# Graph layer on one core: the first twelve gathers read x itself, and messages run 16 instead of 22 units behind

## The chip, the cores and the metric

The kernel runs on one core of a Trainium2 chip. The metric is the time of one execution on the device in microseconds (us), lower is better; it is the median of several runs. Beside the times stands a profile of one execution: what each engine did when, and what ended each of its waits. The engines are TensorE (PE, its weight loads PEld), VectorE (DVE), ScalarE (ACT), GpSimd (POOL) and SyncE (SP, which here only issues DMAs).

## The reference

A pre-normalised graph layer over 6250 nodes with 256 features and 206250 edges (each with 64 features and a polarity). Edges are sorted by destination.

```python
h = relu(layernorm(x))                                   # [6250, 256]
e = relu(raw @ W_e1.T + b_e1) @ W_e2.T + b_e2            # [206250, 256]
edge_emb = (e * (clip(polarity, 0, 1) + 0.01)) @ W_le.T + b_le
msg  = relu(h[src] + edge_emb)
aggr = segment_sum(msg, dst, 6250)
t = (h + aggr) @ W_g1.T + b_g1
out = x + relu(layernorm(t) * ln_g + ln_b) @ W_g2.T + b_g2
```

All data are float32.

## The kernel before

Edges are taken in 403 blocks of 512; a block is two units of 256 edges, 806 units in all (`NU`). W_e2 and W_le are multiplied into one matrix once (`product`, L383), so that a unit costs the following.

- First layer, for a pair of blocks (four units): eight matmuls 64x512 into four PSUM banks (L248), emptied with bias and Relu by ACT (L257, three of them) and DVE (L254, the fourth).
- Second layer, for a unit (`edge_part`, L264): eight matmuls 128x256 (L272), emptied into a `msg` tile by DVE with the bias added (L277). In the prologue every third unit is `plain`: ACT empties it (L275), and the bias is added by DVE when the message is finished (L582).
- Gather: two indirect DMAs for each unit, issued by GpSimd (`gather`, L530, L537). Each fetches 128 rows of 1 KB from `hb_d`, a copy in HBM of relu(layernorm(x)) + b_le.
- Finishing the message (`whole`, L578): DVE multiplies `msg` by the polarity and adds the gathered row, in two instructions 128x256 (L584); ACT applies Relu in place (L589).
- Sums (`add_up`, L591): for each pair of blocks 32 matmuls (L601) with a 0/1 matrix `sel`, which DVE builds from the destinations (L566), add messages of equal destination. Later a further matmul distributes these sums to windows of 128 nodes, and the node layer follows (`node_work`).

The PSUM banks named `pz` come from a pool of seven (`psz`); every result above except the sums goes through it, in the order of the code.

The prologue (L342 to L446) loads x in 13 chunks of up to 512 rows on SP's queue, and for each chunk DVE takes row statistics (L140, L141), ACT a root (L365) and the normalisation with Relu (L375), GpSimd adds b_le (L379), and SP writes the rows to `hb_d` (L381). Since a gather may need any row, no gather starts before the last row is written. Between chunks the first `LEAD` = 22 units are put through both layers (`forward`), and their messages wait in `msg`.

The main loop runs over the units 22 to 805. In each pass a unit goes through the second layer, every fourth unit or pair of pairs brings first layers, sums and loads with it (`turn_of`), and `whole` is called for older units: the lag is `LEAD - u // SHRINK` units, never under one, so 22 at the start and 1 at the end. The order is written out by hand: no scheduler moves instructions, and each engine works through its own in the order of the code. Gathers are handed out in step with TensorE (`in_step`, L549): an estimate of TensorE's time so far, `spent`, divided by `STEP`, says how many may have been issued, each behind a matmul; besides, at most 16 units (`HG`) beyond the summed ones, for which there are buffers.

At the start of the loop a few steps are done once: `first_rows` (L456) and `rows_of_edges` (L464) work out the destinations relative to their strip, which `sel` needs; `row_numbers`, `stats_out` and `node_weights` follow some units later.

Of the kernel before, what the change touches and what calls it, by code (L numbers as in the profile page):

```python
# [17 lines left out]
P = 128  # L18
# [23 lines left out]
EDGE, LAYER, SUMS, NODES = 1.754, 0.9, 0.46, 0.65  # L42
STEP = 1.282
AFLOAT = 6.0
SHRINK = 36
HG = 16
FEW = 6
QUIET = (0, 1)
# [48 lines left out]
def gnn_kernel(ctx: ExitStack, tc: tile.TileContext, x, src_c, dst_c, dst_r, pol_c, raw_t, w_e1t, w_e2,  # L97
# [119 lines left out]
    with fast:  # L217
# [4 lines left out]
        e1_p = big.enter_context(tc.tile_pool(name="e1", bufs=8))  # L222
        msg_p = big.enter_context(tc.tile_pool(name="msg", bufs=LEAD + 2))
        psz = big.enter_context(tc.tile_pool(name="psz", bufs=7, space=PSUM))
        psd = big.enter_context(tc.tile_pool(name="psd", bufs=1, space=PSUM))
# [6 lines left out]
        def load_pair(q):  # L232
            if q < NP:
                raw[q] = ld.tile([P, 512], F32, name="raw")
                nc.sync.dma_start(out=raw[q], in_=raw_t[q])
# [68 lines left out]
        def forward(u):  # L304

            edge_part(u)
            if u % 4 == TURN:
                turn_of(u // 4)
# [12 lines left out]
        vecs = load("vecs", [P, 8], vec_c, nc.scalar)  # L321
        be1_s, be2_s, lng_s, lnb_s = (vecs[:, 2 * i:2 * i + 2] for i in range(4))
        load_pair(0)
        early = ExitStack()
# [9 lines left out]
        for j in range(S):  # L334
            nc.gpsimd.iota(p32[j * W:(j + 1) * W], pattern=[[0, 1]], base=0, channel_multiplier=1,
                           allow_small_or_imprecise_dtypes=True)
        full = NF * L * S
        dst_f = w0.tile([P, NT], F32, name="dst_f")
        be2_b = w0.tile([P, 2, P], F32, name="be2_b")


        with tc.tile_pool(name="p1", bufs=4) as p1, tc.tile_pool(name="p1x", bufs=11) as p1x:  # L342
            parts = list(chunks())
# [23 lines left out]
            def nodes_out(k):  # L367

                t0, p, t = parts[k]
                rs, nm = rs_s[:p, t0:t0 + t], nm_s[:p, t0:t0 + t]  # L370
                nc.vector.reciprocal(rs, rs)
                nc.vector.scalar_tensor_tensor(nm, mvs[k][:p, :t, 0], -1.0, rs, op0=ALU.mult, op1=ALU.mult)
                xt = xts.pop(k)
                for i in range(t):
                    nc.scalar.activation(xt[:p, i, :], xt[:p, i, :], AF.Relu, bias=nm_s[:p, t0 + i:t0 + i + 1],  # L375
                                         scale=rs_s[:p, t0 + i:t0 + i + 1])
                hb = p1.tile([P, CH, D], F32, name="hb")
                for i in range(t):
                    nc.gpsimd.tensor_add(hb[:p, i, :], xt[:p, i, :], ble_b[:p])  # L379
                for a, b in spread_out(p):  # L380
                    nc.sync.dma_start(out=rows(hb_d, t0, p, t)[a:b], in_=hb[a:b, :t])  # L381
# [37 lines left out]
            for k in range(len(parts) + 1):  # L419
# [15 lines left out]
                for _ in range((k > 0) + (k > 2 and k % 3 > 0)):  # L435
                    u = next(units, None)
                    if u is not None:
                        forward(u)
                if k in lists:
                    t, src = lists[k]  # L440
                    nc.scalar.dma_start(out=t, in_=src[:, :NT])
            nc.gpsimd.tensor_copy(dst_f, dst_f.bitcast(I32))
            for u in units:
                forward(u)
            nc.vector.tensor_scalar(pol_s, pol_s, 0.0, 1.0, op0=ALU.max, op1=ALU.min)
            nc.vector.tensor_scalar_add(pol_s, pol_s, 0.01)  # L446
# [74 lines left out]

        with tc.tile_pool(name="hg", bufs=HG) as hg_p, tc.tile_pool(name="ms", bufs=5) as ms_p, \
                tc.tile_pool(name="sel2", bufs=9) as sel2_p, tc.tile_pool(name="nd", bufs=3) as nd:
            got = 0
            acc = {}
# [4 lines left out]
            def gather(behind=None):  # L530
# [4 lines left out]
                if i == 0:  # L535
                    hg[u] = hg_p.tile([P, 2, D], F32, name="hg")
                g = nc.gpsimd.indirect_dma_start(  # L537
# [11 lines left out]
            def in_step(us, behind):  # L549

                nonlocal spent
                spent += us
                while got * STEP < spent + AFLOAT and got < 2 * min(NU, 4 * summed + HG):
                    gather(behind)
                    behind = None
# [22 lines left out]
            def whole(u):  # L578

                m = msg.pop(u)  # L580
                if plain(u):
                    nc.vector.tensor_add(m, m, bc_s)  # L582
# [156 lines left out]

            gathers(1)  # L740
            sums = add_pairs
            paced = in_step
            for i, fn in ((0, first_rows), (1, rows_of_edges), (3, lambda: rest.extend(select(0) + select(1))), (5, row_numbers), (6, stats_out),
                          (8, node_weights)):
                at(LEAD + i, fn)
# [4 lines left out]
            for u in range(LEAD, NU):  # L750
# [6 lines left out]
                piece()  # L757
                while made < u + 1 - max(LEAST, LEAD - u // SHRINK) - (by_two(u // 4) and (u + 1) % 8 == TURN):
                    gathers(made + 1)
                    whole(made)  # L760
                    made += 1
# [208 lines left out]
```

## Time and profile before

| | |
|---|---|
| median of 3 runs | 2550.69 us (2548.15 to 2566.38) |
| the profiled execution | 2558.52 us, its span 2556.8 us |
| granted TensorE clock, mean | 0.965 of full speed |
| busy: PE, DVE, POOL, ACT | 93%, 64%, 64%, 38% of the span |
| prologue, until the last rows are written | 0 to about 62 us |
| first gather issued | 63.65 us |
| first sums on TensorE (L601) | 97.99 us |
| one gather on GpSimd | 0.99 us, 1612 of them |

An engine's busy time is the union of its instructions' durations. In the profile's rows, the part in square brackets is the idle time of the engine just before the instruction and what ended it; "issue" means that the profile shows nothing that was waited for.

### The profile page before, as it was taken

To read this page: it belongs to the slowest core of one execution; us is meant where nothing else is said; L and a number is where in the kernel's file an instruction comes from. 1 tells how busy PE (TensorE), PEld (TensorE's weight loads), DVE (VectorE), ACT (ScalarE), POOL (GpSimd) and SP (SyncE) were. 2 spreads that over 40 slices of the span, in tenths; PEclk is the share of its full clock that TensorE was granted. 3 is DMA by queue.
4 is the path that set the end of the run, shared out by engine and by line. 5 is a ranking of instruction groups with operands and counts; after the bars stand their busy time and mean duration, and the time that the engine had idled before them with its cause. 6 is when DMAs were issued, how large, how long until landed. Compare 5 with 4: busy or idle time off the path is not lost.

```text
span 2556.8 us, 35901 instructions
## 1 busy us (share of the span) xinstructions
PE 2378.9 (93%) x12382; PEld 1670.3 (65%) x12382; DVE 1647.0 (64%) x3953; ACT 980.9 (38%) x1701; POOL 1638.7 (64%) x1675
## 2 busy tenths in 40 slices
PE   9998998999999989999999999999999999899987
PEld 7666666666666757666666666666666666666664
DVE  7776666666666666666656666656666666656655
ACT  7333333343343433334333433433333433333432
POOL 5666666666666666666666666666666665666662
PEclk9999999999999999998999999999999999999998
DMA  8433343334334433433343444334334333343341
GB/s 300 129 115 113 108 134 112 114 114 130 113 108 125 130 119 106 133 108 117 111 144 101 115 126 122 110 106 137 112 114 131 118 107 114 109 131 109 119 119 55
DMA packets 156084, 309.24 MB, mean 121 GB/s; under 512 B 33183, under 2 KB 77944, under 8 KB 155896
## 3 DMA queue, kind: packets, MB, share of 16 engines
q0 software_dynamic: 77376, 211.39, 28.5%
q1 hardware_dynamic: 77364, 92.23, 11.4%
q10 hardware_dynamic: 1156, 3.28, 0.3%
q8 instruction: 98, 1.61, 0.3%
q14 instruction: 90, 0.74, 0.1%
HBM read 293.92 MB, written 12.85 MB: 120 GB/s over the span
## 4 chain that ended last, share of the span: by engine, by line
PE 82%; issue 5%; DVE 5%; another core or an unknown queue 3%; ACT 1%; DVEq 0%; ACTq 0%
PE pz L272 49%; PE pz L248 17%; PE pd L601 9%; PE pz L701 3%; DVE hg L584 2%; PE pz L195 2%; PE pz L169 2%; DVE msg L277 1%; ACT e L257 0%; DVE sel L566 0%; PE pz L185 0%; ACT hg L589 0%; DVE hT L676 0%; DVE e L254 0%
## 5 line engine op out<-in xcount | busy, mean ns | idle before, releaser
L537 POOL DMA_INDIRECT hg<-hb_d,src_s x1612 | 1601.5, 993 | 861.2 <-issue 525.4
L272 PE MATMUL pz<-wc_s,e 128*128 128x256 f32 x6448 | 1486.5, 384 | 51.8 <-issue 38.6
L272 PEld LDWEIGHTS pz<-wc_s,e 128*128 128x128 f32 x6448 | 1216.7, 192 | 318.8 <-issue 99.8
L589 ACT ACTIVATE hg<-hg 128x512 f32<-128x512 f32 x805 | 508.5, 632 | 1117.2 <-DVE hg L584 854.1
L277 DVE TENSOR_TENSOR msg<-pz,bc_s 128x512 f32<-128x512 f32 x799 | 546.6, 686 | 325.1 <-PE pz L272 152.3
L584 DVE SCALAR_TENSOR_TENSOR hg<-msg,pol_s,hg 128x256 f32<-128x256 f32 x1612 | 697.5, 480 | 2.6 <-issue 1.5
L248 PE MATMUL pz<-raw,we_s 64*128 64x512 f32 x1612 | 510.3, 653 | 42.8 <-issue 22.9
L254 DVE TENSOR_SCALAR e<-pz,vecs 128x512 f32<-128x512 f32 x201 | 150.5, 749 | 500.0 <-PE pz L248 201.4
L257 ACT ACTIVATE e<-pz,vecs 128x512 f32<-128x512 f32 x605 | 376.4, 686 | 225.1 <-PE pz L248 84.9
L248 PEld LDWEIGHTS pz<-raw,we_s 64*128 64x128 f32 x1612 | 177.2, 195 | 281.6 <-issue 164.7
L601 PE MATMUL pd<-hg,sel 128*32 128x256 f32 x3216 | 258.6, 408 | 53.1 <-issue 50.9
L601 PEld LDWEIGHTS pd<-hg,sel 128*32 128x32 f32 x3216 | 114.0, 115 | 221.2 <-issue 170.0
L566 DVE SCALAR_TENSOR_TENSOR sel<-iota_w,zero_c,rel 128x128 f32<-128x128 f32 x403 | 138.8, 344 | 0.0
L613 ACT ACTIVATE ms<-pd 128x256 f32<-128x256 f32 x66 | 25.5, 386 | 191.7 <-remote 60.1
L701 PEld LDWEIGHTS pz<-s,ms 128*128 128x128 f32 x548 | 70.3, 194 | 9.1 <-issue 3.8
L701 PE MATMUL pz<-s,ms 128*128 128x128 f32 x548 | 71.7, 278 | 4.7 <-issue 2.5
L676 DVE SCALAR_TENSOR_TENSOR hT<-hT,zero_c,stb 128x128 f32<-128x128 f32 (+1 forms) x196 | 67.2, 343 | 1.7 <-issue 1.7
L169 PE MATMUL pz<-wg_s,hT 128*128 128x256 f32 (+1 forms) x196 | 52.8, 389 | 9.9 <-DVE hT L703 7.4
L195 PE MATMUL pz<-wg_s,nT 128*128 128x256 f32 (+1 forms) x196 | 53.9, 393 | 5.6 <-ACT hg L589 2.7
L169 PEld LDWEIGHTS pz<-wg_s,hT 128*128 128x128 f32 (+1 forms) x196 | 36.5, 191 | 20.0 <-DVE hT L703 9.7
L379 POOL TENSOR_TENSOR hb<-xt,rows_b 128x256 f32<-128x256 f32 (+1 forms) x49 | 34.2, 729 | 23.4 <-DMA xt<-in_x_dram 12.7
L195 PEld LDWEIGHTS pz<-wg_s,nT 128*128 128x128 f32 (+1 forms) x196 | 37.7, 195 | 15.2 <-issue 6.4
(91 smaller groups left out, 393.0 us busy)
## 6 DMA issues: line engine op xcount, KB each, us to landing
raw<-in_raw_t_dram SPq DMA_DIRECT2D x202, 256.0 KB
hg<-hb_d,src_s POOLq DMA_INDIRECT x1612
stb<-st_d SPq DMA_DIRECT2D x49, 128.0 KB
hb_d<-hb SPq DMA_DIRECT2D x12, 512.0 KB
xt<-in_x_dram SPq DMA_DIRECT2D x48, 128.0 KB
hT<-in_x_t_dram SPq DMA_DIRECT2D x48, 128.0 KB
out_dram<-ot SPq DMA_DIRECT2D x48, 128.0 KB
xt<-in_x_dram SPq DMA_DIRECT2D x11, 512.0 KB
```

Source lines behind the costliest of these rows:

```text
L169: nc.tensor.matmul(ph[:n, 0, :], aT[:, c, :n], wg1_s[:, c, :], start=c == 0 and not bias_by_pe, stop=c == 1)
L195: nc.tensor.matmul(po[:n, 0, :], nT[:, c, :n], wg2_s[:, c, :], start=c == 0, stop=c == 1)
L248: z = nc.tensor.matmul(pe[s, c], we1_s[s * F:(s + 1) * F, c * P:(c + 1) * P], raw[q][s * F:(s + 1) * F, :], start=True, stop=True)
L254: nc.vector.tensor_scalar(e1[b][:, c, :], pe[s, c], be1_s[:, c:c + 1], 0.0, op0=ALU.add, op1=ALU.max)
L257: nc.scalar.activation(e1[b][:, c, :], pe[s, c], AF.Relu, bias=be1_s[:, c:c + 1])
L272: last_z = nc.tensor.matmul(pz[:, i, :], e1[b][:, c, k:k + P], wc_s[:, c, :], start=c == 0, stop=c == 1)
L277: nc.vector.tensor_add(msg[u], pz, bc_s)
L537: g = nc.gpsimd.indirect_dma_start(out=hg[u][:, i, :], out_offset=None, in_=hb_d, in_offset=bass.IndirectOffsetOnAxis(ap=src_s[:, 2 * u + ...
L584: nc.vector.scalar_tensor_tensor(hg[u][:, i, :], m[:, i, :], pol_s[:, 2 * u + i:2 * u + i + 1], hg[u][:, i, :], op0=ALU.mult, op1=ALU.add)
L589: nc.scalar.activation(hg[u], hg[u], AF.Relu)
L601: z = nc.tensor.matmul(acc[g][j * W:(j + 1) * W, :], sel[g][:, k * S + j, :], m[:, j % 2, :], start=k == 0, stop=b == blocks_of(g)[-1])
L701: nc.tensor.matmul(pa[:, c, :n], ms[g][:, c * P:(c + 1) * P], box["sel2"][i][:, :n], start=i == 0, stop=i == len(gs) - 1)
```

## The change

- A small index tile `src_0` (12 columns of the source indices) is loaded on ACT's queue between `vecs` and `we2_s`. Before the first chunk is processed, GpSimd issues twelve gathers, those of units 0 to 5 (`RAW` = 6), that read rows of x and not of `hb_d`.
- Behind the last chunk, ahead of the units 20 and 21 of the prologue, DVE takes the statistics of the twelve gathered 128-row blocks; a root, a reciprocal and a product follow, and ACT normalises them in twelve instructions. When one of these six messages is finished, DVE adds b_le to the gathered rows in a further instruction, since `hb_d` would have held it.
- The lag is `LEAD - RAW - u // SHRINK` with `SHRINK` = 50: 16 units at the start and 1 at the end. In the first units of the loop two messages are finished in each pass (`ready_for`), until the lag is reached.
- The other gathers are counted from the thirteenth on, with `STEP` = 1.29.
- `rows_of_edges` and the call of `select` stand in one step, two units sooner than `select` stood before. The cast of the destinations on GpSimd moves from behind the last row addition to a place ahead of the last two.
- Buffers: half of the 16 gather buffers are allocated ahead of the prologue, x has ten chunk buffers instead of eleven, `hb` three instead of four, and the scratch of GpSimd's DMA descriptors is set to 8192 bytes for each partition; the kernel before leaves the default, twice as much.

```diff
@@ -40,10 +40,11 @@
 LEAD = 22
 LEAST = 1
 EDGE, LAYER, SUMS, NODES = 1.754, 0.9, 0.46, 0.65
-STEP = 1.282
+STEP = 1.29
 AFLOAT = 6.0
-SHRINK = 36
+SHRINK = 50
 HG = 16
+RAW = 6
 FEW = 6
 QUIET = (0, 1)
 TURN = 1
@@ -221,6 +222,7 @@
         sel_p = big.enter_context(tc.tile_pool(name="sel", bufs=3))
         e1_p = big.enter_context(tc.tile_pool(name="e1", bufs=8))
         msg_p = big.enter_context(tc.tile_pool(name="msg", bufs=LEAD + 2))
+        hx_p = big.enter_context(tc.tile_pool(name="hx", bufs=HG // 2))
         psz = big.enter_context(tc.tile_pool(name="psz", bufs=7, space=PSUM))
         psd = big.enter_context(tc.tile_pool(name="psd", bufs=1, space=PSUM))
         raw, sel, e1, hg, msg, ms = {}, {}, {}, {}, {}, {}
@@ -320,6 +322,11 @@
         nc.scalar.dma_start(out=we1_s, in_=w_e1t)
         vecs = load("vecs", [P, 8], vec_c, nc.scalar)
         be1_s, be2_s, lng_s, lnb_s = (vecs[:, 2 * i:2 * i + 2] for i in range(4))
+        src_0 = const.tile([P, 2 * RAW], I32, name="src_0")
+        mv_0 = const.tile([P, 2 * RAW, 2], F32, name="mv_0")
+        rs_0 = const.tile([P, 2 * RAW], F32, name="rs_0")
+        nm_0 = const.tile([P, 2 * RAW], F32, name="nm_0")
+        nc.scalar.dma_start(out=src_0, in_=src_c[:, :2 * RAW])
         load_pair(0)
         early = ExitStack()
         w0 = early.enter_context(tc.tile_pool(name="w0", bufs=1))
@@ -334,12 +341,19 @@
         for j in range(S):
             nc.gpsimd.iota(p32[j * W:(j + 1) * W], pattern=[[0, 1]], base=0, channel_multiplier=1,
                            allow_small_or_imprecise_dtypes=True)
+        for u in range(RAW):
+            hg[u] = hx_p.tile([P, 2, D], F32, name="hg")
+            for i in range(2):
+                nc.gpsimd.indirect_dma_start(
+                    out=hg[u][:, i, :], out_offset=None, in_=x,
+                    in_offset=bass.IndirectOffsetOnAxis(ap=src_0[:, 2 * u + i:2 * u + i + 1], axis=0))
         full = NF * L * S
         dst_f = w0.tile([P, NT], F32, name="dst_f")
         be2_b = w0.tile([P, 2, P], F32, name="be2_b")
 
 
-        with tc.tile_pool(name="p1", bufs=4) as p1, tc.tile_pool(name="p1x", bufs=11) as p1x:
+        with tc.tile_pool(name="p1", bufs=4) as p1, tc.tile_pool(name="p1h", bufs=3) as p1h, \
+                tc.tile_pool(name="p1x", bufs=AHEAD) as p1x:
             parts = list(chunks())
             xts, mvs = {}, {}
             units = iter(range(LEAD))
@@ -374,7 +388,7 @@
                 for i in range(t):
                     nc.scalar.activation(xt[:p, i, :], xt[:p, i, :], AF.Relu, bias=nm_s[:p, t0 + i:t0 + i + 1],
                                          scale=rs_s[:p, t0 + i:t0 + i + 1])
-                hb = p1.tile([P, CH, D], F32, name="hb")
+                hb = p1h.tile([P, CH, D], F32, name="hb")
                 for i in range(t):
                     nc.gpsimd.tensor_add(hb[:p, i, :], xt[:p, i, :], ble_b[:p])
                 for a, b in spread_out(p):
@@ -436,12 +450,23 @@
                     u = next(units, None)
                     if u is not None:
                         forward(u)
+                if k == 11:
+                    nc.gpsimd.tensor_copy(dst_f, dst_f.bitcast(I32))
                 if k in lists:
                     t, src = lists[k]
                     nc.scalar.dma_start(out=t, in_=src[:, :NT])
-            nc.gpsimd.tensor_copy(dst_f, dst_f.bitcast(I32))
-            for u in units:
+            for n, u in enumerate(units):
+                for m in range(n * RAW // 2, (n + 1) * RAW // 2):
+                    row_stats(p1, P, 2, lambda i: hg[m][:, i, :], mv_0[:, 2 * m:2 * m + 2, :])
                 forward(u)
+            nc.scalar.activation(rs_0, mv_0[:, :, 1], AF.Sqrt, bias=eps_t)
+            nc.vector.reciprocal(rs_0, rs_0)
+            nc.vector.scalar_tensor_tensor(nm_0, mv_0[:, :, 0], -1.0, rs_0, op0=ALU.mult, op1=ALU.mult)
+            for u in range(RAW):
+                for i in range(2):
+                    k = 2 * u + i
+                    nc.scalar.activation(hg[u][:, i, :], hg[u][:, i, :], AF.Relu, bias=nm_0[:, k:k + 1],
+                                         scale=rs_0[:, k:k + 1])
             nc.vector.tensor_scalar(pol_s, pol_s, 0.0, 1.0, op0=ALU.max, op1=ALU.min)
             nc.vector.tensor_scalar_add(pol_s, pol_s, 0.01)
 
@@ -519,9 +544,9 @@
             nc.vector.tensor_copy(bad_i, pq[:1, 0, 0:1])
 
 
-        with tc.tile_pool(name="hg", bufs=HG) as hg_p, tc.tile_pool(name="ms", bufs=5) as ms_p, \
+        with tc.tile_pool(name="hg", bufs=HG // 2) as hg_p, tc.tile_pool(name="ms", bufs=5) as ms_p, \
                 tc.tile_pool(name="sel2", bufs=9) as sel2_p, tc.tile_pool(name="nd", bufs=3) as nd:
-            got = 0
+            got = 2 * RAW
             acc = {}
             made = 0
             summed = 0
@@ -533,7 +558,7 @@
                 u, i = divmod(got, 2)
                 got += 1
                 if i == 0:
-                    hg[u] = hg_p.tile([P, 2, D], F32, name="hg")
+                    hg[u] = (hx_p if u % HG < HG // 2 else hg_p).tile([P, 2, D], F32, name="hg")
                 g = nc.gpsimd.indirect_dma_start(
                     out=hg[u][:, i, :], out_offset=None, in_=hb_d,
                     in_offset=bass.IndirectOffsetOnAxis(ap=src_s[:, 2 * u + i:2 * u + i + 1], axis=0))
@@ -550,7 +575,7 @@
 
                 nonlocal spent
                 spent += us
-                while got * STEP < spent + AFLOAT and got < 2 * min(NU, 4 * summed + HG):
+                while (got - 2 * RAW) * STEP < spent + AFLOAT and got < 2 * min(NU, 4 * summed + HG):
                     gather(behind)
                     behind = None
 
@@ -578,6 +603,8 @@
             def whole(u):
 
                 m = msg.pop(u)
+                if u < RAW:
+                    nc.vector.tensor_add(hg[u], hg[u], ble_b.rearrange("p (o d) -> p o d", o=1).to_broadcast([P, 2, D]))
                 if plain(u):
                     nc.vector.tensor_add(m, m, bc_s)
                 for i in range(2):
@@ -737,10 +764,14 @@
                 if fns:
                     todo.setdefault(now + 1, deque()).extendleft(reversed(fns))
 
-            gathers(1)
+            gathers(RAW + 1)
             sums = add_pairs
             paced = in_step
-            for i, fn in ((0, first_rows), (1, rows_of_edges), (3, lambda: rest.extend(select(0) + select(1))), (5, row_numbers), (6, stats_out),
+            def strips():
+                rows_of_edges()
+                rest.extend(select(0) + select(1))
+
+            for i, fn in ((0, first_rows), (1, strips), (5, row_numbers), (6, stats_out),
                           (8, node_weights)):
                 at(LEAD + i, fn)
             for i, fn in enumerate((by_group(0, ALU.max), by_group(1, ALU.min), by_row(0, ALU.max), by_row(1, ALU.min),
@@ -755,7 +786,9 @@
                     gathers(4 * summed + HG)
 
                 piece()
-                while made < u + 1 - max(LEAST, LEAD - u // SHRINK) - (by_two(u // 4) and (u + 1) % 8 == TURN):
+                lag = max(LEAST, LEAD - RAW - u // SHRINK) + (by_two(u // 4) and (u + 1) % 8 == TURN)
+                ready_for = min(u + 1 - lag, 2 * (u + 1 - LEAD))
+                while made < ready_for:
                     gathers(made + 1)
                     whole(made)
                     made += 1
@@ -958,7 +991,7 @@
 
         "x_t": laid(np.asarray(x).T.reshape(2, P, N).transpose(1, 0, 2)),
     }
-    nc = bacc.Bacc("TRN2", target_bir_lowering=False, num_devices=1)
+    nc = bacc.Bacc("TRN2", target_bir_lowering=False, num_devices=1, dynamic_dma_scratch_size=8192)
     arrays = {f"in_{k}_dram": a for k, a in ins.items()}
     args = [nc.dram_tensor(k, a.shape, mybir.dt.from_np(a.dtype), kind="ExternalInput").ap()
             for k, a in arrays.items()]
```

## The prediction

> **What bounds the kernel now.** I read the page's busy times and its chain first, then the table of ten-microsecond stretches around the place that is edited, then the timeline of VectorE there.
>
> ```profile
> PE 2378.9 (93%) x12382; PEld 1670.3 (65%) x12382; DVE 1647.0 (64%) x3953; ACT 980.9 (38%) x1701; POOL 1638.7 (64%) x1675
> ...
> PE 82%; issue 5%; DVE 5%; another core or an unknown queue 3%; ACT 1%; DVEq 0%; ACTq 0%
> ```
>
> TensorE sets the time: 93% busy, 82% of the chain that ended last. No other engine passes 64%, and all matrix products of the kernel remain in the changed one (equal instruction counts in the two built programs). So the change cannot shorten TensorE's work; it can only remove waits of TensorE or add some. Next, where are waits? Columns: stretch and length, then busy us (instructions) of PE, PEld, DVE, ACT, POOL, granted clock, DMA share, GB/s.
>
> ```profile
> 20.00:30.00 10.00, 10.00 (x46) 7.56 (x45) 9.03 (x34) 8.67 (x20) 7.57 (x12) 1.00 1.08 380
> 30.00:40.00 10.00, 10.00 (x47) 7.53 (x46) 9.35 (x32) 9.48 (x20) 7.83 (x12) 1.00 1.07 378
> 60.00:70.00 10.00, 10.00 (x46) 7.28 (x45) 6.12 (x9) 2.77 (x6) 6.65 (x5) 1.00 0.57 175
> 70.00:80.00 10.00, 10.00 (x46) 7.16 (x45) 8.68 (x16) 5.49 (x10) 7.90 (x7) 1.00 0.32 93
> 80.00:90.00 10.00, 10.00 (x49) 8.77 (x48) 6.33 (x18) 2.17 (x4) 7.58 (x8) 1.00 0.41 117
> 90.00:100.00 10.00, 7.23 (x32) 2.76 (x35) 7.10 (x16) 2.60 (x5) 5.69 (x6) 0.66 0.55 182
> 110.00:120.00 10.00, 9.92 (x44) 7.38 (x42) 9.93 (x24) 4.09 (x7) 7.73 (x8) 1.00 0.53 165
> ```
>
> TensorE is full up to 90 us, through the end of x's normalisation (near 62 us), the first gather (63.65 us) and the first finished message. A deep backlog of 22 units costs nothing there: there is no hole to fill. At 90 us comes a stall of TensorE's own: single matmuls 0.70 us apart, waiting for no engine. Such stalls return about every 26 us to the end, and weigh the same on both kernels.
>
> ```profile
> 8.11 1.97 PE L388 MATMUL pz<-wle_s,we_s 128*128 128x256 f32 x8 [1.22 <-DMA we_s<-in_w_e_dram]
> ...
> 61.14 0.69 DVE L277 TENSOR_TENSOR msg<-pz,bc_s 128x512 f32<-128x512 f32 x1 [2.76 <-PE pz L272]
> 62.87 0.69 DVE L277 TENSOR_TENSOR msg<-pz,bc_s 128x512 f32<-128x512 f32 x1 [1.03 <-PE pz L272]
> 64.82 0.75 DVE L254 TENSOR_SCALAR e<-pz,vecs 128x512 f32<-128x512 f32 x1 [1.26 <-PE pz L248]
> ...
> 77.31 1.66 DVE L584 SCALAR_TENSOR_TENSOR hg<-msg,pol_s,hg 128x256 f32<-128x256 f32 x4
> 78.89 0.69 DVE L277 TENSOR_TENSOR msg<-pz,bc_s 128x512 f32<-128x512 f32 x1
> ```
>
> The first line: TensorE waits for one weight load early. The others: VectorE has small holes between 57.69 and 78.89 us, 2.76 + 1.04 + 1.26 + 0.40 + 0.47 + 0.83 = 6.8 us in all (its ends against its next starts). 78.89 us is where it empties unit 26's PSUM bank.
>
> **The change, part by part.**
>
> *The index load.* The new load of `src_0` is third on ACT's queue. In the built order W_e2's load now stands where the `rows_b` load stood, behind a wait for the first load's completion lane. W_e2 was issued at 1.87 us; rows_b came out of that wait at 3.77. So W_e2 leaves 1.9 us later, and line 388 waits for it. Behind line 388 TensorE's work is gapless from 13.75 to 62.76 us but for some 0.5 us, so 1.4 to 1.9 us reach the end of the prologue. I take +1.9.
>
> *Twelve gathers at the start.* At 0.99 us busy and 0.30 between two (rows of L537), GpSimd needs 12 x 1.3 = 15.5 us from about 5 us on, so `hb` of chunk 0 (15.17 us before) starts near 21 to 23 us. One chunk takes 2.78 us of each 3.58 us, so 0.8 us is regained per chunk; with some 11 us idle between 15 and 60 us the delay of 6 to 8 us is gone before the last chunk, also with the 1.53 us cast moved ahead of the last two chunks. SP's row writes and raw loads queue behind those additions; raw pairs are loaded four pairs (36 us) ahead, which hides 8 us. Cost 0, and up to +2 if the last write slips. The bytes are 12 x 128 KB = 1.6 MB, 4.2 us at the 380 GB/s of a full stretch; x chunks (1.4 us each at that rate) are used every 3.6 us, so this is hidden.
>
> The Trainium skill, "DMA: Bandwidth & Descriptors", section "Queues, rings and completion order", says that each DMA engine takes turns between the queues that have work. That speaks against the early gathers: by it x's loads get half the rate while gathers are under way, an estimated 4 us of lost x transfer, and if that were not hidden the sum would be 4 us higher; the rows above (2.8 us per chunk at half rate, 3.6 us of use) hide it.
>
> *Statistics of twelve row blocks on VectorE.* Start to start a `bn_stats`/`bn_aggr` pair takes 0.55 us (8.27 to 8.83 us): 12 x 0.55 = 6.6, and 0.4 for reciprocal and product. ACT gets 12 x 0.52 = 6.2 us of Relu where it is a third busy.
>
> *Messages sooner.* In units 22 to 27 two messages per unit are finished instead of one. By unit 26's bank VectorE has finished messages 0 to 7, not 0 to 3: four more at 0.79 = 3.2, two more bias additions (units 4 and 7, L582) at 0.72 = 1.4. Messages 0 to 5 need an added 128x512 addition of `ble`, priced like L582: 6 x 0.72 = 4.3. The strips and the first seven `sel` blocks (0.26 to 0.35 each) now come ahead: 2.1.
>
> Together 6.6 + 0.4 + 3.2 + 1.4 + 4.3 + 2.1 = 18.0 us before that bank, of which holes take 6.8: VectorE is 11.2 us late there. TensorE has seven banks to run ahead in. At unit 25 it meets the first sums, which wait for messages 0 to 3 and `sel`, then four first-layer banks, which wait for the banks of units 23 to 25. Walking VectorE's new order with the durations above, these come free 8 to 14 us later than unit 26 started before (76.54 us). I take 11.2.
>
> *Credits.* TensorE has then done one pair of sums (32 matmuls, 1.93 us) that it did later before: -1.9 (-3.9 if two pairs). While VectorE is behind, TensorE's own stall at 90 us (5.3 us lost) can lie under the same wait: 0 to -5.3, I take half, -2.6. From 109 to 125 us VectorE was full and TensorE idle for 0.9 and 2.1 us behind it; the new order has less there (no `sel`, fewer bias additions): 0 to -3, I take -1.5.
>
> *What moves nothing.* STEP and SHRINK: gathers handed out per unit fall from 1612/784 to 1600/784, and GpSimd is 64% busy; the lead of the gathers over the messages stays 5 to 9 by the code's formula, and both lags end at 1. The rate is 32 units per 100 us both at a lag of 20 and at one of 3, so a lag of 16 buys nothing in the loop. The halved descriptor scratch: at most eight gathers are in flight by their completion lanes, and no row shows a wait for room: 0.
>
> Sum: 1.9 + 11.2 - 1.9 - 2.6 - 1.5 = **+7 us**; ends 1.4 + 8 - 3.9 - 5.3 - 3 = -3 and 1.9 + 13.8 - 1.9 + 2 = +16. On the profiled execution that is 2558.5 + 7 = 2566 us. That execution lies 8 us above the median shown, so for the median 2550.7 + 7 = **2558 us**.
>
> **The rivals.**
>
> *Faster: the backlog was what delayed TensorE in the loop.* For it: the waits list puts 60.5 us of TensorE's waits on emptying banks (L277) and 20.8 on L584, and a smaller lag has fewer units in which two messages are finished (15 instead of 21). If half of the 81 us went, 2558 - 40 = 2518 us. Against: these waits stand right behind TensorE's own stalls, evenly over the run. It decides if waits before L248 shrink after 200 us.
>
> *Slower: the burst finds no cover.* Place: units 20 to 33. If the new work is served in series, because TensorE's first sums stand in its queue ahead of everything that VectorE could empty, holes and stall absorb nothing: 1.9 + 18.0 + 6.2 (ACT's Relus ahead of `base_b`, on which the strips wait) = 26 us, 2577 us, and to 2590 if the gathers, handed out in step with TensorE, fall behind as well. It decides once TensorE starts unit 26 later than about 100 us. For it: VectorE is 87 to 99% full in two of these stretches. Against: seven banks and the holes.
>
> *Slower: the scratch.* 1612 gathers in 2460 us leave 1.53 us each; now 1.29. Were one to cost 0.27 us more, GpSimd would set the time: about 2580 us. No row speaks for it.
>
> *The burst is hidden.* TensorE's own stalls, 5.3 us and more per 26 us, swallow it, and only the credits show: 2549 us.
>
> **How the numbers follow.** Forecast 2558: 0.42; hidden burst 2549: 0.13; both lie within 1%, 2525 to 2576, about what a measurement of this kernel can tell from no change: 0.55. Faster backlog: 0.15. No cover 0.25 and scratch 0.05: 0.30. The forecast's own range is 2548 to 2567. For 8 in 10 I leave out a tenth at either side: 2520 to 2590.
>
> **What would show it.** Right: line 388's counterpart starts near 10 us; VectorE has no idle gap from 58 to 90 us; unit 26's matmuls start 85 to 92 us; the first sums stand near 80 to 87 us instead of 97.99; the loop again runs 32 units per 100 us. Wrong: TensorE full from 62 to 90 us again (hidden), a gap over 20 us there (no cover), gathers over 1.2 us (scratch), or 33 units per 100 us in the loop (backlog).

## The result: 32 us slower

The median went from 2551.44 us (2548.15 to 2566.38, 4 runs) to 2583.26 us (2580.97 to 2586.32, 4 runs): a ratio of 1.0116, 95% interval 1.0090 to 1.0142. The profiled spans, 2556.8 and 2579.2 us, are 22.4 us apart. The time lies inside the range given for 8 in 10, 2520 to 2590 us, but outside the forecast's own range, 2548 to 2567 us; the likeliest value, +7 us, was too small.

The page after (busy times, then the chain that ended last):

```profile
PE 2394.9 (93%) x12382; PEld 1669.3 (65%) x12382; DVE 1660.2 (64%) x3985; ACT 980.4 (38%) x1714; POOL 1627.2 (63%) x1675
...
PE 80%; DVE 9%; issue 5%; another core or an unknown queue 4%; ACT 1%; DMA 1%; SPq 0%; DVEq 0%; ACTq 0%; POOLq 0%
```

TensorE has the same instructions and the same share; VectorE's share of the chain rose from 5 to 9%. The stretches after (columns as before: busy us of PE, PEld, DVE, ACT, POOL, granted clock, DMA share, GB/s):

```profile
20.00:30.00 10.00, 6.66 (x19) 4.62 (x18) 6.03 (x21) 4.27 (x9) 6.49 (x9) 0.68 1.08 354
60.00:70.00 10.00, 10.00 (x47) 7.53 (x46) 7.49 (x24) 7.18 (x15) 7.69 (x10) 1.00 0.56 169
70.00:80.00 10.00, 10.00 (x46) 7.29 (x45) 9.66 (x24) 7.37 (x15) 5.92 (x6) 1.00 0.55 167
80.00:90.00 10.00, 5.80 (x31) 2.00 (x29) 9.88 (x19) 3.52 (x8) 7.87 (x8) 0.76 0.31 91
90.00:100.00 10.00, 8.68 (x22) 5.37 (x21) 8.71 (x22) 5.72 (x10) 3.95 (x4) 0.56 0.19 53
```

Two places are new. From 20 to 30 us TensorE is busy 6.66 us instead of 10.00. From 80 to 90 us it is busy 5.80 us while VectorE is full (9.88), and the granted clock is 0.56 in the next stretch. The timelines of VectorE and TensorE there (the kernel after; L279 empties a unit's bank, L628 are the sums, L591 builds `sel`):

```profile
8.30 1.97 PE L402 MATMUL pz<-wle_s,we_s 128*128 128x256 f32 x8 [0.38 <-PE pz L250]
...
23.66 0.69 DVE L279 TENSOR_TENSOR msg<-pz,bc_s 128x512 f32<-128x512 f32 x1 [8.23 <-remote]
...
80.46 2.21 PE L250 MATMUL pz<-raw,we_s 64*128 64x512 f32 x8
86.87 1.94 PE L628 MATMUL pd<-hg,sel 128*32 128x256 f32 x16 [4.20 <-DVE sel L591]
88.74 2.08 PE L250 MATMUL pz<-raw,we_s 64*128 64x512 f32 x4
92.14 2.44 PE L250 MATMUL pz<-raw,we_s 64*128 64x512 f32 x4 [1.32 <-DVE msg L279]
94.51 5.80 PE L274 MATMUL pz<-wc_s,e 128*128 128x256 f32 x16
```

Unit 0's bank is emptied at 23.66 us instead of 15.75, after 8.23 us for which the profile names no engine ("remote"). Later TensorE stands 4.20 us for `sel`, without which no sum can start, and unit 26's second layer starts at 94.51 us instead of 76.54. Taking for each unit the time at which its bank was emptied, minus the same in the kernel before, gives where the time went: +7.9 us at unit 0, +7.7 at 18, +19.8 at 27, +11.4 at 36, +12.3 at 60, +12.2 at 120, +3.4 at 200, +10.6 at 390, +31.0 at 660 and +22.4 at the last. So some 12 us are lost by unit 36, in the first 110 us; behind it the difference comes and goes by more than 10 us, and two single profiles can't tell where the rest is lost.

### The profile page after: what moved, and what is told of

Its sections match the earlier page's. It is cut to its first block, busy times and chain, and to the rows that moved or that the text cites. A ratio compares the mean times of both kernels' runs of the same rounds, so it can differ in the third digit from the quotient of the medians.

```text
span 2579.2 us, 35856 instructions
## 1 busy us (share of the span) xinstructions
PE 2394.9 (93%) x12382; PEld 1669.3 (65%) x12382; DVE 1660.2 (64%) x3985; ACT 980.4 (38%) x1714; POOL 1627.2 (63%) x1675
## 4 chain that ended last, share of the span: by engine, by line
PE 80%; DVE 9%; issue 5%; another core or an unknown queue 4%; ACT 1%; DMA 1%; SPq 0%; DVEq 0%; ACTq 0%; POOLq 0%
PE pz L274 49%; PE pz L250 16%; PE pd L628 9%; DVE hg L611 3%; DVE msg L279 2%; PE pz L728 2%; PE pz L170 2%; PE pz L196 1%; DMA xt<-in_x_dram 1%; DVE st L141 1%; DVE sel L591 1%; PE pz L186 0%; DVE e L256 0%; ACT e L259 0%
## 5 line engine op out<-in xcount | busy, mean ns | idle before, releaser
L562 POOL DMA_INDIRECT hg<-hb_d,src_s x1600 | 1578.6, 987 | 901.4 <-issue 567.1
L274 PE MATMUL pz<-wc_s,e 128*128 128x256 f32 x6448 | 1505.5, 387 | 64.6 <-issue 55.5
L279 DVE TENSOR_TENSOR msg<-pz,bc_s 128x512 f32<-128x512 f32 x799 | 545.7, 685 | 420.4 <-PE pz L274 168.3
L250 PEld LDWEIGHTS pz<-raw,we_s 64*128 64x128 f32 x1612 | 171.4, 193 | 281.4 <-issue 161.7
L628 PE MATMUL pd<-hg,sel 128*32 128x256 f32 x3216 | 250.2, 414 | 35.8 <-issue 29.4
L628 PEld LDWEIGHTS pd<-hg,sel 128*32 128x32 f32 x3216 | 112.4, 117 | 205.2 <-issue 159.3
L591 DVE SCALAR_TENSOR_TENSOR sel<-iota_w,zero_c,rel 128x128 f32<-128x128 f32 x403 | 138.0, 343 | 0.0
L730 DVE SCALAR_TENSOR_TENSOR hT<-hT,pz 128x256 f32<-128x256 f32 x48 | 20.0, 417 | 81.8 <-PE pz L274 46.0
```

The costliest lines, as they stand in the source:

```text
L250: z = nc.tensor.matmul(pe[s, c], we1_s[s * F:(s + 1) * F, c * P:(c + 1) * P], raw[q][s * F:(s + 1) * F, :], start=True, stop=True)
L274: last_z = nc.tensor.matmul(pz[:, i, :], e1[b][:, c, k:k + P], wc_s[:, c, :], start=c == 0, stop=c == 1)
L279: nc.vector.tensor_add(msg[u], pz, bc_s)
L562: g = nc.gpsimd.indirect_dma_start(out=hg[u][:, i, :], out_offset=None, in_=hb_d, in_offset=bass.IndirectOffsetOnAxis(ap=src_s[:, 2 * u + ...
L591: nc.vector.scalar_tensor_tensor(sel[g][:, k * S:(k + 1) * S, :], iota_w.rearrange("p (o w) -> p o w", o=1).to_broadcast([P, S, W]), zero_ ...
L628: z = nc.tensor.matmul(acc[g][j * W:(j + 1) * W, :], sel[g][:, k * S + j, :], m[:, j % 2, :], start=k == 0, stop=b == blocks_of(g)[-1])
```

## The experiments

Twelve runs of nine kernels were made in four sets (three kernels ran in two sets), each set on a chip of its own, with runs of the kernel before beside them. The chips differ much: the kernel before took 2178.32 us on the first and 2528.12, 2553.77 and 2555.12 us on the three others. On the first chip TensorE is 99% busy and the stalls that fill both profiles above are absent. Only ratios within a set are compared, except where the text names another chip.

**Set 1, the chip without stalls (before 2178.32 us).**

`buffers`, the kernel before with the new buffers and scratch:

```diff
-tc.tile_pool(name="p1x", bufs=11) as p1x
+tc.tile_pool(name="p1h", bufs=3) as p1h, tc.tile_pool(name="p1x", bufs=AHEAD) as p1x
-hb = p1.tile(...)
+hb = p1h.tile(...)
+dynamic_dma_scratch_size=8192
```

> The kernel before with three changes only: the descriptor scratch of 8192 bytes, ten chunk buffers for x instead of eleven, three for hb instead of four. My prediction (these move nothing): 2551 us. Rival S (the scratch makes gathers slower or later): 2560 to 2580 us, with a gather on GpSimd above 1.0 us or more of GpSimd's time spent waiting.

2179.26 us, ratio 1.0002 (0.9993 to 1.0011), a gather 985 ns on GpSimd. On this chip buffers and scratch cost nothing.

`old_lag`, the changed kernel with the lag of the kernel before:

```diff
-lag = max(LEAST, LEAD - RAW - u // SHRINK) + (by_two(u // 4) and (u + 1) % 8 == TURN)
-ready_for = min(u + 1 - lag, 2 * (u + 1 - LEAD))
+ready_for = u + 1 - max(LEAST, LEAD - u // 36) - (by_two(u // 4) and (u + 1) % 8 == TURN)
```

> The changed kernel with the lag of the kernel before (22 units minus u // 36, one message per unit): early gathers, statistics, STEP, buffers and scratch stay. Theory A with the burst priced at some 5 us and the lag in the loop at nothing: 2578 us. Rival E (the smaller lag costs TensorE its cover in the loop): about 20 us less than the changed kernel, 2563 us, with less waiting of the second layer for VectorE's emptying. Rival D (nothing but the early gathers and their statistics): 2583 us.

2179.07 us, ratio 1.0004 (0.9995 to 1.0013). Twelve gathers at the start, statistics, b_le and strips are free here; unit 0 is only 0.5 us later than in `buffers`.

`spread`, the changed kernel with its gathers taken apart:

```diff
-for u in range(RAW): ...            # twelve gathers ahead of the chunks
+if 4 <= k < 4 + RAW:                # two behind each of chunks 4 to 9
+    early_gathers(k - 4)
```

> The changed kernel, but its twelve gathers are issued two at a time behind chunks 4 to 9 instead of back to back at the start; everything else is as in the changed kernel. Theory A (the gathers at the start hold up the loads of x and the first units: unit 0's bank was emptied 7.8 us later): unit 0 is emptied at 16 to 17 us again and the time is about 8 us below the changed kernel, 2575 us. Rival B (the late start comes from the index load on ACT's queue, which is still there, and the gathers cost nothing): unit 0 stays near 24 us, 2583 us. Rival C (gathers cost GpSimd 15 us wherever they stand, and the last row write slips): no gain, or the last hb addition later than 70 us and the time above 2583 us.

2188.15 us, ratio 1.0039 (1.0026 to 1.0053): 9.8 us above the kernel before and 9.1 above `old_lag`, though nothing holds up its first units (+0.6 us at unit 0). Against `buffers` its units are 14.9 us late at 27 and between 7 and 16 us from unit 39 on (9.2 at the last). The changed kernel itself was not run on this chip. TensorE at the first sums, in `buffers`, in `old_lag` and in `spread` (L602, L628 and L631 are the sums):

```profile
95.67 1.12 PE L248 MATMUL pz<-raw,we_s 64*128 64x512 f32 x2
99.09 3.66 PE L248 MATMUL pz<-raw,we_s 64*128 64x512 f32 x6 [2.30 <-DVE msg L277]
102.68 9.70 PE L272 MATMUL pz<-wc_s,e 128*128 128x256 f32 x36
```

```profile
99.01 1.12 PE L250 MATMUL pz<-raw,we_s 64*128 64x512 f32 x2 [0.48 <-DVE msg L279]
100.06 1.94 PE L628 MATMUL pd<-hg,sel 128*32 128x256 f32 x32
...
104.23 8.04 PE L274 MATMUL pz<-wc_s,e 128*128 128x256 f32 x36
```

```profile
84.44 1.94 PE L631 MATMUL pd<-hg,sel 128*32 128x256 f32 x16 [3.81 <-DVE sel L594]
86.31 2.08 PE L250 MATMUL pz<-raw,we_s 64*128 64x512 f32 x4
89.71 2.44 PE L250 MATMUL pz<-raw,we_s 64*128 64x512 f32 x4 [1.33 <-DVE msg L279]
92.08 7.66 PE L274 MATMUL pz<-wc_s,e 128*128 128x256 f32 x24
```

And the stretches of `spread` there:

```profile
80.00:90.00 10.00, 4.86 (x25) 1.26 (x22) 9.89 (x20) 3.06 (x6) 8.12 (x7) 0.65 0.32 93
90.00:100.00 10.00, 10.00 (x31) 7.17 (x31) 8.74 (x22) 5.44 (x10) 7.62 (x8) 0.67 0.32 92
```

This is the price of finishing two messages per unit: waits of 3.81 and 1.33 us, and then matmuls at half clock. Eight first-layer matmuls take 2.08 + 2.44 = 4.5 us instead of 1.99, and 24 of the second layer 7.66 instead of 24 x 8.04 / 36 = 5.4: together 5.1 + 2.5 + 2.3 = 9.9 us. `old_lag` waits 0.48 us and keeps its clock.

`no_early`, units 0 to 5 gathered from `hb_d` like the others, with the new lag (the edit deletes the diff's `src_0`, gathers, statistics and b_le, and counts gathers from the first):

> The changed kernel without the twelve gathers at the start, their index load, statistics, normalisation and the added b_le: units 0 to 5 are gathered from hb_d like the others; the lag of 16, two messages per unit at the start, STEP 1.29, SHRINK 50, the buffers and the scratch stay. Theory A (early gathers 8 us in the prologue, VectorE's 11 us of added work some 4 us): about 12 us below the changed kernel, 2571 us, so that 20 us remain that the lag, STEP or the buffers cost. Rival D (all of the loss comes from the early gathers and their work): 2551 us, like the kernel before. Rival E (the smaller lag or the scratch is all of it): 2583 us or more, since the burst of messages now also waits for gathers that start at 63 us.

2437.22 us, ratio 1.1192 (1.1176 to 1.1207). None of the theories. VectorE waited 563 us for gathered rows: with a lag of 16 and no twelve gathers ahead, each message is due when its rows have just been asked for.

```profile
L588 DVE SCALAR_TENSOR_TENSOR hg<-msg,pol_s,hg 128x256 f32<-128x256 f32 x1612 | 750.0, 482 | 571.8 <-DMA hg<-hb_d,src_s 563.2
```

So it says nothing on the price of the early gathers, but it shows that the shorter lag needs gathers that run further ahead.

**Set 2, a chip with stalls (before 2528.12 us).**

`after_again`, the changed kernel:

> The changed kernel itself, beside the kernel before on the chip of this set of runs. In the first set the kernel before took 2178 us with TensorE busy 99%, without the stalls of some 3 us per 26 us that the two first profiles show. If this set meets that state again, theory A (the burst at units 22 to 27 is what costs, as in the run with spread gathers, +10 us): 2188 us, with one pause of TensorE of some 5 us ahead of the first sums and the granted clock near 0.65 behind it; the late first unit (7.8 us) belongs to the state with the stalls and is not seen again. Rival B (the gathers at the start cost 8 us in every state): 2196 us, unit 0 near 24 us. Rival F (without the stalls the change is free): 2178 us. In the state with stalls: about +20 to +30 us above the kernel before.

2547.34 us, +19.2, ratio 1.0089 (1.0060 to 1.0118); unit 0 is 7.1 us late again.

`ramp`, the changed kernel with the backlog worked off slowly:

```diff
-ready_for = min(u + 1 - lag, 2 * (u + 1 - LEAD))
+ready_for = min(u + 1 - lag, (u + 1 - LEAD) * 9 // 8)
```

> The changed kernel, but the backlog is worked off slowly: ready_for is (u + 1 - LEAD) * 9 // 8 instead of 2 * (u + 1 - LEAD), so one message more in eight units and the lag of 16 is reached after some 48 units. Early gathers, statistics and everything else stay. Theory A (it is the burst): the pause ahead of the first sums is gone and the time is that of the run with the old lag, 2177 to 2180 us. Rival G (the smaller lag costs in the loop, not in its first units): as the changed kernel, about 2188 us.

2558.15 us, +30.0, ratio 1.0121 (1.0102 to 1.0140). On this chip theory A did not hold. The units are 5.1 us late at 36, but 19.2 at 45. GpSimd's timeline shows what came in place of the burst:

```profile
109.86 0.94 POOL L562 DMA_INDIRECT hg<-hb_d,src_s  x1 [8.91 <-ACT hg L616]
...
128.72 0.95 POOL L562 DMA_INDIRECT hg<-hb_d,src_s  x1 [0.30 <-issue]
139.37 0.94 POOL L562 DMA_INDIRECT hg<-hb_d,src_s  x1 [9.71 <-ACT e L259]
```

Gathers now pause for 9 us and then follow each other without a gap, 16 from 109.86 to 128.72 us: they are counted twelve ahead, while the messages that free their buffers are not yet sooner. TensorE's next stop, with 1.63 us and more without a releaser, begins near 126.6 us, behind the fourteenth of them. That the gathers caused it is not shown.

`no_stats`, without statistics, normalisation and b_le of the early rows (units 0 to 5 use bare rows of x):

> The changed kernel without the statistics, the normalisation and the added b_le of the twelve early gathered row blocks (units 0 to 5 use bare rows of x, so this leaves out part of the computation): VectorE is relieved of 6.6 + 0.4 + 4.3 = 11.3 us and ACT of 6.2 us, while the two messages per unit and the earlier strips stay. Theory H (the statistics and b_le fill VectorE, the messages alone would fit): no pause ahead of the first sums, 2178 us. Rival I (two messages per unit and the strips are enough to stop TensorE): still some 5 us of pause, about 2184 to 2188 us.

2545.95 us, +17.8, ratio 1.0089 (1.0058 to 1.0119), as the changed kernel. VectorE is still 9.78 us busy from 80 to 90 us, TensorE 8.23 instead of 5.58 (`after_again`): the pause shrinks, the time does not. This set can't tell a few us from the stalls' own play.

**Set 3, another chip with stalls (before 2553.77 us).** `after_3` is the changed kernel, `spread_2` and `old_lag_2` are the kernels of set 1, `spread_old` has both of their edits.

> The changed kernel itself again, as the measure for the other three kernels of this set. On a chip where the loop stalls (the kernel before near 2530 to 2550 us): about 19 to 30 us above the kernel before, unit 0 emptied 7 us late. On a chip without the stalls (2178 us), theory A (burst): +9 to +10 us, 2188 us, unit 0 on time; rival F (free without the stalls): 2178 us.

> The changed kernel with its twelve gathers issued two at a time behind chunks 4 to 9. Where the loop stalls, theory J (twelve gathers back to back beside the loads of x hold up the completion signals of the engines, which the engines show as remote waits from 15 to 24 us; it needs that state of the chip): unit 0 is on time and the time falls by 5 to 8 us below the changed kernel of this set. Rival K (the 7 us of the prologue are regained in the loop, whose stalls set the time): no difference. Rival B (index load): unit 0 still late. Without the stalls: +10 us as in the first set.

> The changed kernel with the lag of the kernel before, 22 units minus u // 36 and one message per unit. Where the loop stalls: theory L (burst and prologue add): 4 to 6 us below the changed kernel of this set; rival E (a smaller lag leaves TensorE and VectorE less to do while one of them is held up): 12 to 20 us below, as the kernel before or within 7 us of it; rival G2 (the lag is not the cause; the prologue and the statistics are): equal to the changed kernel. Without the stalls: 2179 us as in the first set.

> Both at once: the gathers behind chunks 4 to 9, and the lag of the kernel before. Only the statistics, the b_le additions, the earlier strips, the count of gathers (twelve further ahead) and the buffers remain of the change. Where the loop stalls: theory L: 3 us above the kernel before or less; rival M (STEP and the twelve gathers ahead, which load the DMA engines sooner, cost in the loop): 10 us or more above it remain. Without the stalls: 2177 to 2180 us.

| kernel | median us | ratio to before, 95% interval | unit 0 | unit 36 | unit 120 | last unit |
|---|---|---|---|---|---|---|
| `after_3` | 2583.43 | 1.0125 (1.0098 to 1.0152) | +7.8 | +9.4 | +12.6 | +12.6 |
| `spread_2` | 2587.83 | 1.0139 (1.0117 to 1.0160) | +1.3 | +9.9 | +11.5 | +23.6 |
| `old_lag_2` | 2878.30 | 1.1257 (1.1228 to 1.1286) | +8.5 | +1.2 | +69.1 | +331.3 |
| `spread_old` | 2877.23 | 1.1251 (1.1215 to 1.1287) | +0.8 | +0.2 | +67.9 | +323.7 |

(The last four columns are the times at which a unit's bank was emptied, against the first profile of before.) Two things follow. Taking the gathers apart brings unit 0 back to time and gains nothing at the end: rival K. And the program that was free on the first chip costs 324 us here, which no theory had. By the units' times 69 us are lost by unit 120, 225 by unit 390 and 322 by unit 660; behind that hardly any are added. The waits of `old_lag_2`:

```profile
DVE msg L279 <- remote: 382.3, 83, 11.5
PEld pz L274 <- issue: 311.7, 330, 3.3
PE pz L274 <- issue: 216.7, 248, 3.0
```

TensorE and its weight loads stand for 217 and 312 us with no engine to wait for, and VectorE 382 us for "remote". TensorE's and GpSimd's timeline at one such place:

```profile
150.23 0.59 PE L274 MATMUL pz<-wc_s,e 128*128 128x256 f32 x2 [0.72 <-issue]
152.35 1.32 PE L274 MATMUL pz<-wc_s,e 128*128 128x256 f32 x4 [1.53 <-issue]
154.50 0.46 PE L274 MATMUL pz<-wc_s,e 128*128 128x256 f32 x1 [0.84 <-issue]
...
153.33 0.95 POOL L562 DMA_INDIRECT hg<-hb_d,src_s  x1 [0.30 <-issue]
154.72 0.95 POOL L562 DMA_INDIRECT hg<-hb_d,src_s  x1 [0.44 <-remote]
164.21 0.95 POOL L562 DMA_INDIRECT hg<-hb_d,src_s  x1 [8.54 <-ACT e L259]
```

Gathers follow each other 0.3 us apart from 135.15 us on. TensorE runs beside the first eleven of them without a gap; from 150.23 us on it gets only seven matmuls done in 4.7 us, and then the granted clock falls (0.55 and 0.50 in the two stretches from 155 to 161 us); the gathers pause from 155.7 us on, and at full clock TensorE is again without a gap from 161.8 us. In `old_lag_2` 893 of 1612 gathers stand in rows of eight or more that start less than 1.4 us apart; in the kernel before 424, in the changed one 550. At the median message its gathers are 6 units ahead (before 4.5, `after_3` 5). All 16 units of buffers are taken at times in each of these kernels.

**Set 4, another chip with stalls (before 2555.12 us).** `old_pace`, the changed kernel with lag and count of the kernel before:

```diff
-STEP = 1.29
+STEP = 1.282
-while (got - 2 * RAW) * STEP < spent + AFLOAT and ...
+while got * STEP < spent + AFLOAT and ...
-lag = ...
-ready_for = min(u + 1 - lag, 2 * (u + 1 - LEAD))
+ready_for = u + 1 - max(LEAST, LEAD - u // 36) - (by_two(u // 4) and (u + 1) % 8 == TURN)
```

> The changed kernel with the lag of the kernel before and with its count of gathers too (STEP 1.282, got * STEP instead of (got - 12) * STEP), so that the twelve early gathers are no lead: in the loop gathers and messages stand as in the kernel before. Early gathers, statistics, b_le additions, strips, buffers and scratch stay. On a chip where the loop stalls (the kernel before 2520 to 2555 us): theory N (the 324 us of the run with the old lag come from gathers that run twelve ahead of the messages, fill the 16 gather buffers and then follow each other back to back): the loss is gone, 5 to 10 us above the kernel before, GpSimd's gathers 3 to 6 units ahead of the messages; that would leave the lag and STEP as the source of the change's remaining 10 to 15 us. Rival O (scratch, buffers or statistics cost in the loop): 20 to 30 us above the kernel before. Rival Q (the long lag itself, with the early units, costs): 2870 us. Without the stalls: 2179 us by every theory.

2554.88 us, ratio 1.0005 (0.9987 to 1.0024): as the kernel before. This agrees with theory N: with the count and STEP taken back the loss of 324 us is absent, rows of eight or more gathers hold 411 of them, and the lead at the median message is 4 units. `old_lag_2` ran on another chip, so this rests on the kernel before being level on the two (2553.77 and 2555.12 us). The time is better than expected: unit 0 is 7.7 us late again, and at unit 60 0.3 us of it are left. Early gathers, statistics, b_le, strips, buffers and scratch together cost nothing that can be measured, here too. What the change loses lies, by this, in the edits that `old_pace` takes back: the lag with its burst, and the count of gathers with STEP. The changed kernel was not run on this chip; on the two others with stalls it lost 19 and 30 us.

## Why the prediction was right or wrong, step by step

The forecast was 2558 us, 25 us too low. That the time lies between 2520 and 2590 us owes much to luck: three terms put at nothing (the late start, the slow clock behind the pause, the loop) were not nothing, and in part cancelled against a stop of the kernel before. Of the signs named for being right one came true, the first sums at 86.87 us. Line 388's counterpart started at 8.30 and not near 10 us, VectorE was busy for only 7.49 us from 60 to 70 us, and unit 26 started at 94.51 us, behind the 85 to 92 us.

- *Index load, +1.9.* Wrong. W_e2 was issued at 4.02 us instead of 1.87, but line 402 started at 8.30 instead of 8.11. Before, TensorE had waited 1.22 us for that load, whose last part landed at 7.97 us. Now the row puts its 0.38 us down to a matmul, but in the trace its wait for the semaphore of that load ends at 8.25 us, just ahead of line 402. So the load was issued 2.15 us later and awaited only some 0.2 us longer. Term: +0.2.
- *Early gathers, 0.* That they cost nothing in the end holds (`old_pace`, `old_lag`), the working does not. Where the loop stalls, the first units were 6.9 to 8.5 us late. The x loads did lose rate (4.26 MB on q1 from 12 to 24 us before), but on the chip without stalls just as much. From 12 to 24 us, in the changed kernel and in `old_lag` on the first chip (packets, MB, share of the DMA engines; q1 carries x, q0 the gathers):

```profile
q1 hardware_dynamic: 2772, 2.99, 76.2%
q0 software_dynamic: 468, 1.29, 31.0%
```

```profile
q1 hardware_dynamic: 2644, 2.87, 72.2%
```

  (q0 there: 1.30 MB, 31.0%.) Nearly the same shares gave 7.9 us of delay on one chip and 0.5 on the other, so lost transfer time alone is not the cause. The Trainium skill's rule that DMA engines take turns between queues ("DMA: Bandwidth & Descriptors", section "Queues, rings and completion order") agrees with this trace as far as x lost about what the gathers moved, 1.3 MB; the 4 us estimated from it did not show by themselves (0.5 us at unit 0 in `old_lag`). In the changed kernel's trace seven semaphore updates of TensorE, due from 15.8 to 21.4 us by the ends of their matmuls, stand at 23.57 to 23.92 us, one behind the other, and VectorE goes on at 23.66: late completion signals, while gathers follow each other to 21.24 us. In `old_lag`, and in `spread_2` on a chip with stalls, each such update stands within 0.05 us of its matmul's end. Why they are late on some chips was not found. The delay is gone by unit 60 because the kernel before has a stop behind it that `old_pace` has not at that place: `old_pace` is 11.9 us late at unit 28, 5.5 at 29 and 1.4 at 34.
- *The stop at 90 us.* The prediction took it for a stall of TensorE's own, and the rows of the kernel before bear that out:

```profile
82.04 8.37 PE L272 MATMUL pz<-wc_s,e 128*128 128x256 f32 x38
92.14 0.38 PE L272 MATMUL pz<-wc_s,e 128*128 128x256 f32 x1 [1.73 <-issue]
93.55 0.58 PE L272 MATMUL pz<-wc_s,e 128*128 128x256 f32 x1 [1.03 <-issue]
```

  VectorE stands there for 6.09 us, also without a releaser. In `buffers`, on the chip without stalls, the same layer runs without a gap up to the first sums. The 2.30 us ahead of 99.09 us in `buffers` are another stop, behind the first sums: VectorE, itself waiting for gathered rows (1.74, 1.15 and 0.69 us), empties a bank late, and the clock is at half behind it. That one is a wait of the schedule.
- *The burst, +11.2 before credits.* Right in size. Unit 26 started 18.0 us late, of which 7.7 came from the start, so 10.3. On the chip without stalls `spread` lost 11.0 us against `old_lag` by the units' times, 9.1 in the medians.
- *The credits, -1.9, -2.6 and -1.5.* These terms were mis-sized. One pair of blocks is 16 sums matmuls, 0.97 us at full clock; the 32 of the working, and of the description of the kernel, are two pairs. The 0.9 and 2.1 us read as idle time of TensorE near 120 us are those of its weight loads; its matmuls stood 1.25 us behind VectorE. The stop at 90 us gave back more than 2.6 us: the changed kernel is 20.8 us late at unit 28 and 11.4 at unit 36, while the kernel before stands. But `old_pace`, without the burst, gets as much from it (11.9 to 1.4), so by these runs the late start that was priced at nothing used up what the burst was to get. On the chip without stalls nothing comes back: `spread` is 7.9 us behind `old_lag` at unit 27, 10.0 at 36 and 11.0 at the last. Against the credits stands a cost that the working lacks, the slow clock behind the pause. The rows: 0.65 and 0.67 in the two stretches of `spread`, 4.8 us of slow matmuls there. The Trainium skill, "TensorE: Matmul & The Clock Gate", section "HAM oscillation — how this bites in real kernels", gives the rule that TensorE must not idle longer than about 3.4 us. `spread`'s 3.81 us agree; but in `buffers` 2.30 us were enough (0.50 from 101 to 105 us), so here the measurement is the stricter.
- *The loop, 0.* Right on the chip without stalls: the loss of `spread` against `buffers` does not grow after unit 30. Where the loop stalls, the medians lie 19 to 32 us above the kernel before, so some 10 to 20 us remain if the burst costs 10 there too; `ramp`, without the burst, lost 30. `old_pace` shows that they belong to lag or count and not to buffers, scratch or statistics. Which of the two, and how, stays open; more gathers in long rows (485 to 550 in the profiles of the changed kernel against 424) point the way of `old_lag_2` but don't prove it. A count over the traces points there too. TensorE's idle stretches without a releaser, 60 of over 0.6 us in the kernel before, begin in two of three cases at the fifth or a later gather of a row, where only a quarter of the time lies; in `old_lag_2` it is three of four against a third. "TensorE's own stalls weigh the same on both kernels" was wrong as a rule: in `old_lag_2` another order of gathers goes with 324 us more.
- *The rivals.* Scratch: gathers took 987 ns, wrong. Backlog: waits on L279 grew from 60.5 to 71.6 us, wrong. Hidden burst: wrong. No cover: its sign, unit 26 after 100 us, was not reached (94.51), and its price of 26 us for the first units was not paid: 11.4 us are left at unit 36. That the time lies in its range of 2577 to 2590 us is luck; the rest was lost in the loop.

No version was faster than the kernel before: `old_pace`, `old_lag` and the kernel before are level in their own sets.

## What to carry over

How far gathers run ahead and how far messages lag are one number: move both or none. Twelve gathers too few cost 259 us on the chip without stalls (`no_early`); twelve too many cost 324 us on a chip with stalls (`old_lag_2`) and nothing on the first. When work is put on an engine ahead of the first result that the bounding engine needs, price the pause with the slow clock behind it, and when a stop of the kernel before is set against it as a credit, ask what else could use that stop up first. And compare an idle stretch with a second run or chip before saying what it belongs to: the stop at 90 us was gone on the chip without stalls, and another stood 6 us behind its place.

## What was not expected of the hardware

- One program, four chips: 2178.32, 2528.12, 2553.77 and 2555.12 us. On the slower ones engines wait for "issue" and "remote" (101 us for VectorE's L277 in the first profile of before; no such wait of VectorE among the twelve longest of `buffers` on the first chip).
- These stalls go with the order of gathers. The same `old_lag` took 1.0004 of the kernel before on one chip and 1.1257 on another.
- On the first chip rows of eight or more gathers hold 1210 of 1612 in `old_lag`, and TensorE does not stall. Long rows alone are not the cause; something of the chip has to be there, which these runs don't explain.
